# Edge masks read from five copies, a fetched tile in every sixth step, and the on-chip tile's keys behind its step's others

## The chip, the cores and the metric

The kernel runs on one core of a Trainium2 chip. The metric is device time of one launch in microseconds (us), the median of three runs. The profile is one execution more, with its own time. The core has five engines with queues of their own: TensorE (PE), VectorE (DVE), ScalarE (ACT), GpSimd (POOL) and SyncE (SP), and 16 DMA engines which carry the transfers that SP, ACT and POOL issue.

## The reference

A graph layer with five relation types: N = 3125 nodes, E = 100,000 edges sorted by destination, width 128, 8 heads. Each type has its own Q, K and V projections; the softmax runs over the edges of one type that share a destination.

```python
for r in range(R):
    mask = edge_types == r
    q = jnp.einsum('eh,khd->ekd', x_dst, W_Q[r])
    k = jnp.einsum('eh,khd->ekd', x_src, W_K[r])
    v = jnp.einsum('eh,khd->ekd', x_src, W_V[r])
    logits = (q * k).sum(-1) / scale + attn_bias[r][None, :]
    masked_logits = jnp.where(mask[:, None], logits, NEG)
    max_v = jax.ops.segment_max(masked_logits, dst, num_segments=n)
    ...
    exp_l = jnp.where(mask[:, None], jnp.exp(masked_logits - max_v[dst]), 0.0)
    sum_exp = jax.ops.segment_sum(exp_l, dst, num_segments=n)
    attn = exp_l / (sum_exp[dst] + 1e-12)
    out = out + jax.ops.segment_sum(attn[:, :, None] * v, dst, num_segments=n)
out = out.reshape(n, HIDDEN) @ out_proj_w.T + out_proj_b
h = out + node_embeddings
# layer norm of h with gamma and beta; then layernorm(x + that)
```

## The kernel before

Edges are taken in 196 groups of 512 (GE), a group in four tiles of 128 edges (T = 4, P = 128). The main loop has 66 steps (NST): two groups in the first and the last, three groups (12 tiles) in each of the 64 between. A step k also treats the first tile of step k+1, so that a block of 12 tiles (128 x 1536 values of K and as many of V) is one tile later than its groups.

The first 105 us or so prepare tables in HBM: kv_d (K and V of each node and type, a row of 1 KB), q_d (queries), key_d (which destination an edge has, as a number inside its window), and msk_d (a row of 642 bf16 marks for each group, by which the running maxima start anew at each destination; MW = 642). Then each step does the following.

- **POOL** gathers K and V of a tile of 128 edges with one indirect DMA (L849), into one of four buffers: step k into buffer k % 4, of which three lie in the tile kv_early and the fourth in kv_late. `point(k, j, leave)` stands at 11 places of a step (POINTS) and lets gathers go up to a number worked out from its place: 3.0 steps ahead (KV_LEAD) at the start of the program, falling to 2.0 at its end. `leave` is the instruction behind which they are let go.
- Two kinds of tiles aren't gathered. The first tile of steps 3 to 65 is made on chip: PE projects its nodes, and `early_keep` (L1109, ACT) copies the 128 x 256 result into the tile's place. And in one step of eight (PERIOD = 8: steps 11, 19, ..., 59, the table OWN_AT) one tile, `own`, is fetched row by row: `own_fetch` issues 16 DMAs of 1 KB (ROWS) on SP in each of the eight steps before, 128 in all for a tile, and `own_copy` (ACT, L883) puts it into place. The row's address is a register that SP loads from the table rows_at.
- **SP**, behind the products of step k (`take(k)`): `fetch_masks(k+2)` (tile mk, L936: three rows of msk_d, each to 40 partitions, one for each of five types and eight heads), `fetch_keys(k+3)` (tile kt, L719: 128 copies of the step's keys), `fetch_rows(k+3)` (tiles qw, L743: three windows of queries, at addresses that SP loads from the table window), then `own_fetch(k)`. All of them are on SP's one queue.
- **DVE**: products K x q of the step (L975), their sums by head (L1033), masks by type (L1008), norm of an earlier step (L1211 on), `weigh` (weights x V, L1160), the scans for the running maxima (L1115, L1119, which read mk), and `spot(k+2)` (L729), which compares kt with the row number and gives the one-hot matrix from which PE spreads the queries of step k+2 over its edges (L953).
- **PE** turns logits (L1065), spreads queries, turns weights, and sums weighted values by destination (L1194); **ACT** takes exponentials and makes the places matrices for the sums.

The order on each engine is the order in which the code stands (a manual schedule), with semaphores between the engines. A DMA that SP issues signals one of eight semaphores in turn; the next one that uses the same semaphore waits for it first.

Because the tile on chip is the first of the next step's buffer, it lies next to the 11 others only where step k and k+1 have neighbouring buffers. In 32 of the steps (k % 4 being 2 or 3) products and sums are two instructions each, one for 11 tiles and one for one tile.

Of the kernel before, what the change touches and what calls it, by code (L numbers as in the profile page):

```python
# [19 lines left out]
P = 128  # L20
# [3 lines left out]
R = 5  # L24
# [34 lines left out]
LANES = R * HEADS  # L59
L3 = G3 * LANES  # L60
# [8 lines left out]
PERIOD = 8  # L69
# [80 lines left out]
def windowed_path(  # L150
# [22 lines left out]
    msk_d = dram.tile([NGR, MW], BF16, name="msk_d")  # L173


    def keep(name, shape, dt=F32):
        return const.tile(shape, dt, name=name)
# [7 lines left out]
    rows_at = keep("rows_at", [HG, 2, P], I32)  # L185
# [11 lines left out]
    def kv_tile(name, n):  # L197
        pool = ctx.enter_context(tc.tile_pool(name=f"pool_{name}", bufs=1))
        return pool.tile([P, n * T * G3, KVW], F32, name=name)
# [361 lines left out]
    def own_rows():  # L561
        nc.vector.tensor_scalar_mul(rows_at, kvrow[:, :, P : 2 * P], float(KVW * 4))
# [100 lines left out]
    def late_x():  # L663
# [15 lines left out]
        11: [keys_b],  # L679
        12: [sorted_rows],  # L680
        13: [masks_a],
# [54 lines left out]

    def fetch_rows(k, leave=None):
        a, b = G0[k] + (k > 0), min(G0[k + 1] + 1, NGR)
        bytes_ = q_d.rearrange("n h -> (n h)").bitcast(U8)
        for g, f in zip(range(a, b), starts(window, a, b, SPE)):  # L740
            live["qw", g] = qw = ahead.tile([P, 3, H], BF16, name="qw", bufs=QWB)
            behind(
                nc.sync.dma_start(  # L743
                    qw.rearrange("p s h -> p (s h)").bitcast(U8),
                    bytes_[bass.ds(f, P * WINB)].rearrange("(p h) -> p h", h=WINB),
                ),
                leave,
            )

# [47 lines left out]
    begins()  # L797
    spills()
# [21 lines left out]

    def runs(a, b):
        out_ = []
        for q in range(a, b):
            k = AT[q // T][0]
            kv, at = place(k)
            at += q - T * G0[k]
            if out_ and out_[-1][0] is kv and out_[-1][2] == at:
                out_[-1][2] += 1
            else:
                out_.append([kv, at, at + 1])  # L830
        return out_
# [27 lines left out]
    def own_fetch(k):  # L859
        at = (k - 2) // PERIOD * PERIOD + PERIOD + 3  # L860
        if at not in OWN_AT:
            return
        i = (k - 2) % PERIOD * ROWS
        if i == 0:
            live["own", at] = flow.tile([P, KVW], F32, name="own")
        n = min(ROWS, P - i)
        g = OWN_AT[at] // T
        bytes_ = kv_d.rearrange("n h -> (n h)").bitcast(U8)
        _, rows = nc.values_load_multi_w_load_instructions(
            rows_at[g % HG : g % HG + 1, g // HG, i : i + n], engines=[SPE], min_val=0,  # L870
            max_val=(N * R - 1) * KVW * 4,
            skip_runtime_bounds_check_because="sources are nodes, types are relations",
        )
        for p, f in enumerate(rows, i):
            nc.sync.dma_start(
                live["own", at][p : p + 1].bitcast(U8).rearrange("o (a b) -> o a b", a=2),
                bytes_[bass.ds(f, KVW * 4)].rearrange("(o a b) -> o a b", o=1, a=2),
            )
# [52 lines left out]
    def fetch_masks(k, leave=None):  # L931
        n = len(groups(k))
        live["mk", k] = mk = flow.tile([L3, MW], BF16, name="mk", bufs=3)
        rows = msk_d[G0[k] : G0[k] + n]
# [3 lines left out]
                bass.AP(tensor=rows.tensor, offset=rows.offset, ap=[[MW, n], [0, LANES], [1, MW]]),  # L938
            ),
            leave,  # L940
        )
# [165 lines left out]
    def early_keep(k):  # L1107
        ((kv, c0, _),) = runs(B0[k + 1] - 1, B0[k + 1])
        nc.scalar.copy(kv[:, c0, :], live.pop("rows"))  # L1109
# [298 lines left out]
    fetch_rows(2)  # L1408

# [13 lines left out]
    for k in range(NST - 1):  # L1423
# [24 lines left out]
        if k < NST - 2:  # L1448
# [3 lines left out]
            if k >= 2:  # L1452
                own_fetch(k)
# [662 lines left out]
```

## Time and profile before

| | |
|---|---|
| Median of three runs | 1010.77 us (1009.69 to 1012.93) |
| The profiled execution: its time, its span | 1009.02 us, 1007.2 us |
| Granted TensorE clock, mean | 0.979 |
| Gathers on POOL (L849) | 712 |
| Fetches on SP of single rows (L875) | 896, of 1.0 KB |
| Moved by DMA | 189.60 MB, 188 GB/s |

The span is the time from the first to the last instruction in the trace. The profile gives busy time for each engine, groups of instructions by line, waits with what ended them, the DMA queues (q0 are POOL's gathers, q1 most of what SP issues), and a timeline. In a row of the timeline, the first number is the start, the second the duration (of several in a row, from the first's start to the last's end), and in brackets the idle time ahead of it. In a group's row, busy time and mean of one stand behind the first bar, idle time ahead of them and its causes behind the second.

### The profile page before, as it was taken

How to read it: one execution, taken by the hardware profiler on the slowest of the kernel's cores; microseconds unless marked ns; L12 is line 12 of the kernel's file. 1: busy time of each engine (PE TensorE's matmuls, PEld its weight loads, DVE VectorE, ACT ScalarE, POOL GpSimd, SP SyncE). 2: the span in 40 equal slices, each digit the busy share in tenths (PEclk: the TensorE clock that was granted, in tenths of full speed). 3: DMA queues.
4: the chain of work that ended last, by engine and by line, in shares of the span. 5: the costliest groups of instructions: out<-in, count | busy, mean ns of one | idle time of the engine just before them, and what ended most of it. 6: DMA issues, size and time to landing. Idle time of an engine off the chain costs nothing.

```text
span 1007.2 us, 23071 instructions
## 1 busy us (share of the span) xinstructions
PE 926.2 (92%) x6983; PEld 717.2 (71%) x6983; DVE 899.2 (89%) x1517; ACT 716.3 (71%) x1956; POOL 741.2 (74%) x793
## 2 busy tenths in 40 slices
PE   7995689999999999999999999999999999999986
PEld 3553577777777777777777777778777777777774
DVE  3666788999999999999999999999999999899997
ACT  2443377777787787778777777778777777777765
POOL 7777777777777777777777777777777777777760
PEclk9996799999999999999999999999999999999998
DMA  8997766567666666666666667665666765666630
GB/s 210 356 355 252 206 159 194 158 198 194 177 194 182 179 175 194 177 195 195 177 167 193 195 177 194 178 191 171 193 177 193 194 191 161 185 195 176 160 100 11
DMA packets 100547, 189.60 MB, mean 188 GB/s; under 512 B 19901, under 2 KB 61201, under 8 KB 100298
## 3 DMA queue, kind: packets, MB, share of 16 engines
q0 software_dynamic: 36192, 97.50, 34.9%
q1 hardware_dynamic: 63032, 89.66, 29.7%
q10 hardware_dynamic: 1194, 0.92, 0.4%
q8 instruction: 56, 0.92, 0.4%
q14 instruction: 73, 0.60, 0.2%
HBM read 157.61 MB, written 30.40 MB: 187 GB/s over the span
## 4 chain that ended last, share of the span: by engine, by line
DVE 39%; PE 24%; DMA 21%; issue 8%; POOL 4%; ACT 3%; DVEq 0%; POOLq 0%; ACTq 0%
DMA kv_early<-kv_d,idx 16%; DVE qe L1033 7%; DVE kv_early L975 6%; PE both L1194 5%; PE pr L514 4%; DVE wv L1160 4%; DVE run L1115 4%; DVE run L1119 3%; POOL kv_early L849 3%; PE qe L953 3%; DVE kv_late L975 2%; PE mid L1102 2%; DVE lx L1008 2%; DMA kv_late<-kv_d,idx 2%; PE lt L1092 2%
## 5 line engine op out<-in xcount | busy, mean ns | idle before, releaser
L849 POOL DMA_INDIRECT kv_early<-kv_d,idx x543 | 515.4, 949 | 166.6 <-issue 85.1
L1194 PE MATMUL both<-wv,at 128*125 128x136 f32 x1528 | 261.6, 296 | 0.0
L1173 ACT ACTIVATE at<-wide_at,nkey 128x125 f32<-128x125 f32 x776 | 245.0, 388 | 0.0
L1194 PEld LDWEIGHTS both<-wv,at 128*125 128x125 f32 x1528 | 201.8, 187 | 49.9 <-issue 44.4
L849 POOL DMA_INDIRECT kv_late<-kv_d,idx x169 | 160.0, 947 | 51.5 <-issue 27.1
L1102 PE MATMUL mid<-wkv,xr 128*128 128x256 f32 x630 | 146.5, 379 | 1.6 <-ACT xr L1096 1.6
L953 PE MATMUL qe<-qw,hot 128*128 128x128 bf16 x2349 | 146.1, 222 | 0.0
L953 PEld LDWEIGHTS <-hot 128*128 128x128 bf16 x2352 | 141.6, 102 | 0.5 <-DVE vio L650 0.4
L1102 PEld LDWEIGHTS mid<-wkv,xr 128*128 128x128 f32 x630 | 115.0, 190 | 15.0 <-ACT xr L1096 1.9
L1177 ACT ACTIVATE at<-at 128x500 f32<-128x500 f32 x194 | 120.3, 620 | 6.1
L975 DVE TENSOR_TENSOR kv_early<-kv_early,qe 128x1536 f32<-128x1536 f32 (+3 forms) x70 | 89.3, 1277 | 27.2 <-DMA kv_early<-kv_d,idx 22.0
L1115 DVE TENSOR_TENSOR_SCAN run<-mk,lt 120x640 f32<-120x640 bf16 (+1 forms) x66 | 97.6, 1478 | 1.5 <-PE lt L1065 1.5
L1259 ACT COPY oT<-fin 128x25 f32 x188 | 33.9, 180 | 81.9 <-PE fin L1255 77.9
L1119 DVE TENSOR_TENSOR_SCAN run<-lt,run 120x576 f32<-120x576 bf16 (+1 forms) x65 | 88.2, 1357 | 2.2
L1033 DVE TENSOR_REDUCE qe<-kv_early 128x96 f32<-128x1536 f32 (+2 forms) x65 | 86.7, 1334 | 2.2
L1160 DVE TENSOR_TENSOR wv<-kv_early,mid 128x1536 f32<-128x1536 f32 (+2 forms) x51 | 86.1, 1691 | 1.8 <-PE mid L1102 1.5
L1092 PE MATMUL lt<-diag,xg 128*128 128x512 f32 x252 | 83.5, 454 | 0.0
L1065 PE MATMUL lt<-ident,lx 128*120 128x128 f32 (+2 forms) x396 | 54.7, 275 | 24.6 <-DVE lx L1008 8.6
L1065 PEld LDWEIGHTS lt<-ident,lx 128*120 128x120 f32 (+2 forms) x396 | 38.5, 136 | 52.7 <-ACT diag L1086 20.2
L1144 PEld LDWEIGHTS mid<-gather_heads,ls 120*128 120x128 f32 (+1 forms) x528 | 64.2, 191 | 16.1 <-ACT xTq L901 12.1
L1144 PE MATMUL mid<-gather_heads,ls 120*128 120x24 f32 (+1 forms) x528 | 67.0, 265 | 9.4 <-ACT xTq L901 7.2
L1189 PE MATMUL both<-wv,over 128*5 128x136 f32 x380 | 75.3, 280 | 0.0
(232 smaller groups left out, 1341.5 us busy)
## 6 DMA issues: line engine op xcount, KB each, us to landing
kt<-key_d SPq DMA_DIRECT2D x64, 384.0 KB
qw<-q_d SPq DMA_DIRECT2D x196, 96.0 KB
kv_d<-kvs SPq DMA_DIRECT2D x24, 640.0 KB
own<-kv_d SPq DMA_DIRECT2D x896, 1.0 KB
q_d<-q SPq DMA_DIRECT2D x25, 480.0 KB
mk<-msk_d SPq DMA_DIRECT2D x64, 150.5 KB
kv_early<-kv_d,idx POOLq DMA_INDIRECT x543
kv_late<-kv_d,idx POOLq DMA_INDIRECT x169
```

Source lines behind the costliest of these rows:

```text
L849: nc.gpsimd.indirect_dma_start(out=kv[:, at, :], out_offset=None, in_=kv_d[:, :], in_offset=bass.IndirectOffsetOnAxis(ap=idx[:, q % T, q / ...
L953: spread = nc.tensor.matmul(dest[j], hot[:, j * P : (j + 1) * P], qw[:, c, :], start=(c == 0), stop=(c == 2),)
L975: made = nc.vector.tensor_tensor(kv[:, c0:c1, :H], kv[:, c0:c1, :H], qe[:, n:m], op=ALU.mult)
L1033: made = nc.vector.tensor_reduce(lg[:, n : n + c1 - c0], heads(kv[:, c0:c1, :H]), AX.X, ALU.add)
L1102: nc.tensor.matmul(rows, xr[:, r * P : (r + 1) * P], wkv[:, r].rearrange("h s c -> h (s c)"), start=(r == 0), stop=(r == R - 1),)
L1115: there = nc.vector.tensor_tensor_scan(run[:n], mk[:n, 1 : WIDE + 1], lt, -BIG, op0=ALU.add, op1=ALU.max)
L1119: back = nc.vector.tensor_tensor_scan(run[:n, SEG:][:, ::-1], masks[:, SEG:][:, ::-1], run[:n, SEG:][:, ::-1], -BIG, op0=ALU.add, op1=ALU.max,
L1144: nc.tensor.matmul(ex.rearrange("p (i t) k -> p t i k", t=T)[:, t], ls[: n * LANES, t * P : (t + 1) * P], gather_heads[: n * LANES, :n], s ...
L1160: return nc.vector.tensor_tensor(heads(wv[:, a:b, :H]), heads(kv[:, at + a : at + b, H:]), ex[:, a:b, :, None].to_broadcast([P, b - a, HEA ...
L1173: nc.scalar.activation(at[:, t, :], row_at[:, :WR], AF.Abs, bias=nkey[:, t, g : g + 1], scale=1.0)
L1177: return nc.scalar.activation(at[:, :n], at[:, :n], AF.Relu, bias=1.0, scale=-1.0)
L1194: nc.tensor.matmul(pp[:WR], at[:, t, :], wv[:, T * i + t, :], start=(t == 0), stop=(t == end))
```

## The change

Three edits.

1. A table many_d holds each group's masks five times over. In step 1, `copy_masks` issues one DMA on SP from msk_d to many_d, for all groups from step 6 on (COPIED): 179 rows read, 895 written, 1284 B each. From step 6 on, `fetch_masks` reads 15 rows of many_d, each to eight partitions, where it read three rows, each to 40.
2. PERIOD is 6: the tile fetched row by row is that of steps 9, 15, ..., 63 (ten), with 22 DMAs a step. SP's two loads of addresses in a step (three windows, 16 rows) become one, of a row of a new table at_step with 25 numbers, read by `load_step(k + 4)` behind the third row of the burst. The table is put together ahead of the loop, by a store to row_d and loads from it.
3. Each kv buffer has one column more. K of the tile made on chip is kept behind the others of its step (`beyond`), V where it was. `early_keep` makes two copies of 128 x 128 where these lie apart. `products` and `logits` are then one instruction in every inner step.

The core of the diff:

```diff
 LANES = R * HEADS
+COPIES = 5
+COPIED = 6
 L3 = G3 * LANES
...
 QWB = 10
...
 FAR = 4000
-PERIOD = 8
+PERIOD = 6
 ROWS = -(-P // PERIOD)
...
 KVA = 3
...
     msk_d = dram.tile([NGR, MW], BF16, name="msk_d")
+    many_d = dram.tile([NGR, COPIES, MW], BF16, name="many_d")
+    row_d = dram.tile([HG * 2 * P + P], I32, name="row_d")
...
     def keep(name, shape, dt=F32):
...
     window = keep("window", [1, NGR], I32)
-    rows_at = keep("rows_at", [HG, 2, P], I32)
+    at_step = keep("at_step", [NST, G3 + ROWS], I32)
     oT = keep("oT", [P, N + WN])
...
     gamma_t = keep("gamma_t", [P, H])
...
         pool = ctx.enter_context(tc.tile_pool(name=f"pool_{name}", bufs=1))
-        return pool.tile([P, n * T * G3, KVW], F32, name=name)
+        return pool.tile([P, n * T * G3 + 1, KVW], F32, name=name)
...
...
     def own_rows():
-        nc.vector.tensor_scalar_mul(rows_at, kvrow[:, :, P : 2 * P], float(KVW * 4))
+        rows_at = srt.rearrange("g s i -> g (s i)").bitcast(I32)[:, : 2 * P]
+        nc.vector.tensor_scalar_mul(
+            rows_at.rearrange("g (s i) -> g s i", s=2), kvrow[:, :, P : 2 * P], float(KVW * 4)
+        )
+        nc.sync.dma_start(
+            row_d[: HG * 2 * P].rearrange("(g i) -> g i", g=HG), rows_at
+        )
+
+    def own_steps(i):
+        def run():
+            for k in list(OWN_AT)[i::4]:
+                g = OWN_AT[k] // T
+                a, f = (g % HG * 2 + g // HG) * P, k - PERIOD - 1 + 3
+                nc.sync.dma_start(
+                    at_step[f : f + PERIOD, G3:],
+                    row_d[a : a + PERIOD * ROWS].rearrange("(i j) -> i j", j=ROWS),
+                )
+        return run
+
+    def window_steps():
+        nc.sync.dma_start(
+            at_step[3 : NST - 1, :G3],
+            window[:, G0[3] + 1 : G0[NST - 1] + 1].rearrange("o (k j) -> o k j", j=G3),
+        )
...
...
         10: [lambda: along(kvrow, 1, put_idx)],
-        11: [keys_b],
-        12: [sorted_rows],
-        13: [masks_a],
+        11: [keys_b, own_steps(0)],
+        12: [sorted_rows, own_steps(1)],
+        13: [masks_a, own_steps(2), own_steps(3)],
         14: [masks_b],
...
         16: [short_rows],
...
+    def load_step(k):
+        if not 3 <= k < NST - 1:
+            return
+        own = own_part(k - 3)
+        n = own[2] if own else 0
+        _, at = nc.values_load_multi_w_load_instructions(
+            at_step[k : k + 1, : G3 + n], engines=[SPE], min_val=0,
+            max_val=(N * R - 1) * KVW * 4,
+            skip_runtime_bounds_check_because="rows of nodes, sources and types",
+        )
+        live["at_step", k] = [
+            nc.s_assert_within(
+                f, 0, (N - 1) * R * WINB,
+                skip_runtime_bounds_check_because="destinations are nodes",
+            )
+            for f in at[:G3]
+        ] + list(at[G3:])
+
     def fetch_rows(k, leave=None):
...
         bytes_ = q_d.rearrange("n h -> (n h)").bitcast(U8)
-        for g, f in zip(range(a, b), starts(window, a, b, SPE)):
+        if 3 <= k < NST - 1:
+            at = live.pop(("at_step", k))
+            live["rows_at", k - 3] = at[G3:]
+        else:
+            at = starts(window, a, b, SPE)
+        for g, f in zip(range(a, b), at):
             live["qw", g] = qw = ahead.tile([P, 3, H], BF16, name="qw", bufs=QWB)
...
                 nc.sync.dma_start(
...
             )
+
+    def own_part(k):
+        at = (k - 2) // PERIOD * PERIOD + PERIOD + 3
+        if k < 2 or at not in OWN_AT:
+            return None
+        i = (k - 2) % PERIOD * ROWS
+        return at, i, min(ROWS, P - i)
...
...
     begins()
+    window_steps()
     spills()
...
     project_weights()
...
+    def beyond(k):
+        kv, at = place(k)
+        return kv, at + T * G3
+
     def runs(a, b):
...
             k = AT[q // T][0]
-            kv, at = place(k)
-            at += q - T * G0[k]
+            if q == T * G0[k] and k - 1 in early_at:
+                kv, at = beyond(k - 1)
+            else:
+                kv, at = place(k)
+                at += q - T * G0[k]
             if out_ and out_[-1][0] is kv and out_[-1][2] == at:
...
             else:
...
     def own_fetch(k):
-        at = (k - 2) // PERIOD * PERIOD + PERIOD + 3
-        if at not in OWN_AT:
+        rows = live.pop(("rows_at", k), None)
+        if not rows:
+            load_step(k + 4)
             return
-        i = (k - 2) % PERIOD * ROWS
+        at, i, n = own_part(k)
         if i == 0:
             live["own", at] = flow.tile([P, KVW], F32, name="own")
-        n = min(ROWS, P - i)
-        g = OWN_AT[at] // T
         bytes_ = kv_d.rearrange("n h -> (n h)").bitcast(U8)
-        _, rows = nc.values_load_multi_w_load_instructions(
-            rows_at[g % HG : g % HG + 1, g // HG, i : i + n], engines=[SPE], min_val=0,
-            max_val=(N * R - 1) * KVW * 4,
-            skip_runtime_bounds_check_because="sources are nodes, types are relations",
-        )
         for p, f in enumerate(rows, i):
+            if p == i + G3:
+                load_step(k + 4)
             nc.sync.dma_start(
...
                 bytes_[bass.ds(f, KVW * 4)].rearrange("(o a b) -> o a b", o=1, a=2),
...
         live["mk", k] = mk = flow.tile([L3, MW], BF16, name="mk", bufs=3)
-        rows = msk_d[G0[k] : G0[k] + n]
+        c = COPIES if k >= COPIED else 1
+        rows = (many_d if c > 1 else msk_d)[G0[k] : G0[k] + n]
         behind(
...
                 mk[: n * LANES, :],
-                bass.AP(tensor=rows.tensor, offset=rows.offset, ap=[[MW, n], [0, LANES], [1, MW]]),
+                bass.AP(
+                    tensor=rows.tensor, offset=rows.offset,
+                    ap=[[MW, n * c], [0, LANES // c], [1, MW]],
+                ),
             ),
             leave,
+        )
+
+    def copy_masks():
+        nc.sync.dma_start(
+            many_d[G0[COPIED] :],
+            msk_d[G0[COPIED] :, None, :].to_broadcast([NGR - G0[COPIED], COPIES, MW]),
         )
...
     def spread_q(k):
...
     def early_keep(k):
-        ((kv, c0, _),) = runs(B0[k + 1] - 1, B0[k + 1])
-        nc.scalar.copy(kv[:, c0, :], live.pop("rows"))
+        rows, (kv, c0), (to, c1) = live.pop("rows"), beyond(k), place(k + 1)
+        if kv is to and c0 == c1:
+            nc.scalar.copy(kv[:, c0, :], rows)
+        else:
+            nc.scalar.copy(kv[:, c0, :H], rows[:, :H])
+            nc.scalar.copy(to[:, c1, H:], rows[:, H:])
...
         n = len(groups(k)) * LANES
...
     fetch_rows(2)
+    load_step(3)
...
         if k + 2 < NST:
...
             take(k, made)
-            if k >= 2:
-                own_fetch(k)
+            own_fetch(k)
+            if k == 1:
+                copy_masks()
             point(k - 1, 7, weighted)
```

Instructions on SP, where the copy stands: step 1's last row fetches and step 2 up to its own rows, first before (L936 is the mask fetch, L875 the own rows).

```order
L936 DMA mk<-msk_d 120x1x642 [waits DMAHW1_49,DVE_49]
L719 DMA kt<-key_d 128x1536 [waits DMAHW2_49]
L704 TENSOR_LOAD window
L743 DMA qw<-q_d 128x768 [waits DMAHW3_49,PE_49]
L743 DMA qw<-q_d 128x768 [waits DMAHW4_49,PE_49]
L743 DMA qw<-q_d 128x768 [waits DMAHW5_49,PE_49]
L869 TENSOR_LOAD rows_at
L875 DMA own<-kv_d 1x1024 [waits DMAHW6_49]
```

And now (L998 is the mask fetch, L746 the keys, L793 the queries, L936 the own rows; a name like DMAHW5 is one of the eight semaphores):

```order
L769 TENSOR_LOAD at_step [waits DMAHW2_49]
L1009 DMA many_d<-msk_d 895x1x642 [waits DMAHW5_49]
L998 DMA mk<-msk_d 120x1x642 [waits DMAHW6_49,DVE_49]
L746 DMA kt<-key_d 128x1536 [waits DMAHW7_49]
L793 DMA qw<-q_d 128x768 [waits DMAHW0_49,PE_49]
L793 DMA qw<-q_d 128x768 [waits DMAHW1_49,PE_49]
L793 DMA qw<-q_d 128x768 [waits DMAHW2_49,PE_49]
L936 DMA own<-kv_d 1x1024 [waits DMAHW3_49]
L936 DMA own<-kv_d 1x1024 [waits DMAHW4_49]
L936 DMA own<-kv_d 1x1024 [waits DMAHW5_49]
L769 TENSOR_LOAD at_step
```

The copy stands ahead of step 2's fetches in SP's queue; its semaphore is the one that the third own row behind it waits for (DMAHW5), and the one load of addresses stands behind that row.

On DVE, the products and sums of step 2 and the instructions behind them, before:

```order
L975 TENSOR_TENSOR kv_early<-kv_early,qe 128x11x128
L975 TENSOR_TENSOR kv_late<-kv_late,qe 128x128
L1033 TENSOR_REDUCE qe<-kv_early 128x88
L1033 TENSOR_REDUCE qe<-kv_late 128x8
L1008 TENSOR_TENSOR lx<-qe,shut 128x3x4x40
```

and now (L1046 are the products, L1104 the sums):

```order
L1046 TENSOR_TENSOR kv_early<-kv_early,qe 128x12x128
L1104 TENSOR_REDUCE qe<-kv_early 128x96
L1079 TENSOR_TENSOR lx<-qe,shut 128x3x4x40
L1286 TENSOR_SCALAR both<-both 125x16
L1288 RECIPROCAL den<-both 125x16
```

Four instructions of 11 tiles and one have become two of twelve. Over the program DVE's queue has 2260 rows in place of 2324, ACT's 1809 in place of 1774.

## The prediction

> **What bounds the kernel now.** I read the page first: busy time, the DMA queues, the chain's shares, the costliest groups.
>
> ```profile
> span 1007.2 us, 23071 instructions
> PE 926.2 (92%) x6983; PEld 717.2 (71%) x6983; DVE 899.2 (89%) x1517; ACT 716.3 (71%) x1956; POOL 741.2 (74%) x793
> q0 software_dynamic: 36192, 97.50, 34.9%
> q1 hardware_dynamic: 63032, 89.66, 29.7%
> DVE 39%; PE 24%; DMA 21%; issue 8%; POOL 4%; ACT 3%; DVEq 0%; POOLq 0%; ACTq 0%
> L849 POOL DMA_INDIRECT kv_early<-kv_d,idx x543 | 515.4, 949 | 166.6 <-issue 85.1
> L849 POOL DMA_INDIRECT kv_late<-kv_d,idx x169 | 160.0, 947 | 51.5 <-issue 27.1
> ```
>
> PE and DVE have the largest busy shares, and the chain leans on DVE. But POOL's 74% hides a pattern: 712 gathers of 0.95 us, each with idle time ahead of it. So next the timeline of POOL, at the first gather, at the 69th and 70th, and near the end.
>
> ```profile
> 84.72 0.94 POOL L849 DMA_INDIRECT kv_early<-kv_d,idx  x1 [0.30 <-issue]
> 169.34 0.94 POOL L849 DMA_INDIRECT kv_early<-kv_d,idx  x1 [0.30 <-issue]
> 170.59 0.95 POOL L849 DMA_INDIRECT kv_early<-kv_d,idx  x1 [0.30 <-DVE kv_early L975]
> 974.49 0.94 POOL L849 DMA_INDIRECT kv_early<-kv_d,idx  x1 [1.33 <-DVE kv_early L975]
> 976.99 0.94 POOL L849 DMA_INDIRECT kv_early<-kv_d,idx  x1 [0.30 <-issue]
> ```
>
> A gather takes 0.95 us and 0.30 us of issue: 1.25 us from start to start (169.34 to 170.59). From first to last, (976.99 - 84.72)/711 = 1.255 us. So POOL is back to back for 892 us, whatever the busy share says, and DVE waits for what it lands (the waits):
>
> ```profile
> DVE kv_early L975 <- DMA kv_early<-kv_d,idx: 22.0, 24, 1.7
> DVE kv_early L975 <- DMA kv_late<-kv_d,idx: 2.7, 2, 1.6
> ```
>
> About 25 us in 26 waits, all under 2 us: DVE is a little faster than POOL and loses the difference there. The last of these waits is in the timeline of DVE for the end:
>
> ```profile
> 945.21 1.62 DVE L975 TENSOR_TENSOR kv_early<-kv_early,qe 128x1408 f32<-128x1408 f32 x1 [1.48 <-DMA kv_early<-kv_d,idx]
> 958.98 1.62 DVE L975 TENSOR_TENSOR kv_late<-kv_late,qe 128x1408 f32<-128x1408 f32 x1
> 970.18 0.68 DVE L975 TENSOR_TENSOR kv_early<-kv_early,qe 128x512 f32<-128x512 f32 x1
> ```
>
> The step at 945.21 (step 62) still waits for a gather; steps 63 to 65 don't. So POOL sets the time up to 945, DVE and PE the 62 us behind it. What shortens DVE before step 62 is worth nothing; a gather less before it is worth 1.25 us.
>
> **The change, part by part.** Sums are against the profiled execution, 1009.02 us with a span of 1007.2; the median of the runs is 1010.77, 1.75 more, which I add at the end.
>
> *Own tiles.* With a period of 6, the tiles fetched row by row are those of steps 9, 15, ..., 63 (10) in place of 11, 19, ..., 59 (7). Three gathers leave POOL. Up to step 62 it is nine against seven, so the gathers of that step land 2 x 1.25 = 2.5 us sooner. Cost on SP: 22 rows a step in place of 16. One cycle of SP:
>
> ```profile
> 485.04 0.75 SPq L936 DMA_DIRECT2D mk<-msk_d  x1
> 485.84 0.46 SPq L719 DMA_DIRECT2D kt<-key_d  x1
> 487.40 1.41 SPq L743 DMA_DIRECT2D qw<-q_d  x3
> 489.95 6.78 SPq L875 DMA_DIRECT2D own<-kv_d  x16
> 496.83 0.38 SPq L692 DMA_DIRECT2D q_d<-q  x1
> 497.87 0.74 SPq L936 DMA_DIRECT2D mk<-msk_d  x1
> ```
>
> 16 rows took 6.78 us, 0.42 each; six more are 2.5. The two register loads are the gaps 486.30 to 487.40 and 488.81 to 489.95, 1.1 us each; one of them goes, the other now stands behind the third row. From 485.04 to 497.21 SP is taken for 12.2 us, and would be for 12.2 + 2.5 - 1.1 = 13.6. A step of POOL is 11 gathers less one in six for the own tile, 10.83 x 1.25 = 13.6 us. So SP just fits. Part of the 0.42 is waiting for earlier landings, which doesn't grow with the rows, so I take it as hidden; the upper end is a rival. The ten more transfers of the preamble that set up the table lie on SP beside POOL's other gathers; I cost them at nothing, and the cover is small (84.72 must not move). If they held the first gather, the loss would be theirs one for one: up to 10 x 0.46 us (a transfer's issue at 485.84) = 4.6.
>
> *On-chip keys.* These rows are DVE by shape:
>
> ```profile
> L1033 DVE TENSOR_REDUCE qe<-kv_early 128x96 f32<-128x1536 f32 x31 | 54.6, 1761 | 1.1
> L975 DVE TENSOR_TENSOR kv_early<-kv_early,qe 128x1536 f32<-128x1536 f32 x31 | 54.4, 1753 | 16.9 <-DMA kv_early<-kv_d,idx 14.6 <-ACT xTq L901 1.2 <-issue 1.0
> L1033 DVE TENSOR_REDUCE qe<-kv_late 128x88 f32<-128x1408 f32 x16 | 26.0, 1627 | 0.6
> L975 DVE TENSOR_TENSOR kv_late<-kv_late,qe 128x1408 f32<-128x1408 f32 x16 | 25.9, 1619 | 1.9 <-DMA kv_late<-kv_d,idx 0.7 <-DMA kv_early<-kv_d,idx 0.6 <-issue 0.4
> L1033 DVE TENSOR_REDUCE qe<-kv_late 128x8 f32<-128x128 f32 x16 | 4.7, 295 | 0.6
> L975 DVE TENSOR_TENSOR kv_late<-kv_late,qe 128x128 f32<-128x128 f32 x16 | 4.5, 280 | 0.0
> ```
>
> A split step costs 1619 + 280 + 1627 + 295 = 3821 ns, a whole one 1753 + 1761 = 3514: 0.31 us less in 32 steps, 9.8 us of DVE. But up to step 62 that goes into the waits for gathers; only the steps in the tail (62 and 63) give it, 2 x 0.31 = 0.6 us. ACT pays with two copies for one in 32 steps:
>
> ```profile
> L1109 ACT COPY kv_early<-mid 128x256 f32<-128x256 f32 x47 | 16.6, 353 | 0.0
> L901 ACT COPY xTq<-mid 128x128 f32<-128x128 f32 x21 | 5.5, 264 | 5.0 <-PE mid L896 3.6
> ```
>
> 2 x 264 - 353 = 0.18 us a step, on an engine busy for 71%: nothing.
>
> Without the masks the sum is -2.5 - 0.6 = **-3.1 us**.
>
> *Masks.* From step 6 on, a step's masks are read from five copies. What a fetch loads on the DMA engines shows a stretch that has no other transfer on q1 (the DMA view, 281.65 to 283.1):
>
> ```profile
> q0 software_dynamic: 16, 0.05, 57.1%
> q1 hardware_dynamic: 76, 0.08, 17.6%
> ```
>
> 0.176 x 16 = 2.8 engines carry it, though it writes 120 partitions: it has three source rows. With 15 it would take more engines and land sooner; nothing in the waits stands on mk, so that is worth nothing, or a little less delay of gathers beside it, which POOL's pace hides.
>
> The price is the copy itself: one transfer in step 1, 895 rows of 1284 B, 1.149 MB, in SP's queue. [...] The page's q1 moves 89.66 MB in 0.297 x 16 x 1007.2 = 4786 engine-us, 18.7 KB/us; so 1149/18.7 = 61 us. (The window gives 0.08 MB/(0.176 x 16 x 1.45) = 19.6 KB/us, 59 us.) Spread over 16 engines it would be 3.8 us. [...]
>
> [...]
>
> Who stands behind it? SP in step 2 and DVE in steps 3 and 4:
>
> ```profile
> 118.78 0.77 SPq L936 DMA_DIRECT2D mk<-msk_d  x1
> 119.61 0.41 SPq L719 DMA_DIRECT2D kt<-key_d  x1
> 121.12 1.31 SPq L743 DMA_DIRECT2D qw<-q_d  x3
> 131.45 0.77 SPq L936 DMA_DIRECT2D mk<-msk_d  x1
> 132.28 0.41 SPq L719 DMA_DIRECT2D kt<-key_d  x1
> 153.25 0.90 DVE L729 TENSOR_SCALAR hot<-kt,row_of 128x512 bf16<-128x512 bf16 x3
> 155.41 1.75 DVE L975 TENSOR_TENSOR kv_early<-kv_early,qe 128x1536 f32<-128x1536 f32 x1 [0.93 <-DMA kv_early<-kv_d,idx]
> ```
>
> The copy is issued at about 123, behind step 1's qw. Step 2's mk, kt and qw (131.45 on) follow in the same queue; each has some rows on the engine that the copy holds, and a transfer has landed only with its last row. The third row of step 2's own burst also waits for the copy's semaphore. That kt is of step 5, and DVE needs it at 153.25, in step 3. The copy ends at 123 + 61 = 184 if alone; then kt's rows and the spot, 0.9 + about 3 us: 188. Meanwhile DVE stands, and POOL may go only so far ahead: its gathers are let go by the products of the step (releaser at 170.59). The last one that step 3 lets go is the one at 169.34; the next needs products(4), which stand behind the spot. So POOL loses 188 - 170.6 = 17.4 us. DVE is later by 188 - 154.15 = 34 us, of which 17 are its lead, and wins that back over 60 steps from the slack of its 25 us of waits and the 9.8 us above. The end moves by 17.4 - 3.1 = **+14.3 us**.
>
> Bounds of this term: at 24 KB/us (a quarter above the mean) the copy ends at 171 and the spot at 175, a loss of 4.4 and a sum of +1.3; if gathers take a third of that engine, as q0's 34.9% says, the copy lasts up to 61/0.65 = 94 us and the sum is about +47. The gathers' own shares on it are small and mean-rate figures hold such sharing already, so I stay near 61.
>
> Queue order on the engine is what makes kt wait. [...] Were it otherwise, the sum would be -3.1, as in the second case below.
>
> **Rivals.** (a) *The copy is spread, or overtaken, and nothing stalls*: the only case that ends faster. For it: 179 rows on the source side are many; the steps before 153.25 have 30 us of slack from 123, and POOL has 47. Against: the 2.8 engines. It decides at a copy of about 43 us, so two engines would do. Then -3.1: 1009.02 to 1005.9, a median of 1007.7. (b) *SP becomes the bound*: its 13.6 us of work meets a step of 13.6. Each 0.1 us over costs 6 us in 60 steps; at 13.75, with no stall, +9 - 3 = about +6 to 8: 1017 to 1019. For it: the cycle's sum has no slack. Against: the rows' waits, which don't grow. (c) *A short stall*, spot done between 171 and 177: the gain and the loss cancel, within 3 us of before. (d) *Landings*: with lighter mask fetches gathers land sooner (21% of the chain is DMA). POOL's pace bounds it at 3 x 1.25 = 3.8; it adds less than 1 us to (a).
>
> **How the numbers follow.** About 0.3%, 3 us, is what a measurement of this kernel can tell from no change. The stall on one engine has 0.66: 1009.02 + 14.3 = 1023.3, plus 1.75 is 1025; its own range is 1015 to 1036. (a) with (d) 0.22, of which 0.13 passes 3 us; (b) 0.06; (c) 0.06. Slower: 0.66 + 0.06 less 0.04 for stalls that come out short, 0.68; faster 0.14; same 0.18. To leave out no more than 2 in 10 the range must hold (a): 1006.5 to 1036.
>
> **What would show it.** In the profile after: the row of the copy's landing, tens of us, at a steady 15 to 25 GB/s of additional flow on 1/16 of the engines; in step 3 of DVE a wait of some 34 us of the spot for kt; on POOL one gap of some 17 us near 170, and none elsewhere; 709 gathers with 1.25 us between; L1046 with 1536 elements in all inner steps; the mask fetch on some 14 engines. If DVE has no wait at 153, the one-engine reading is wrong and (a) holds. If POOL shows gaps in all steps and SP none, it is (b).

## The result: 34 us slower, and the profile after

| | before | after |
|---|---|---|
| Median | 1011.02 us (1009.16 to 1012.93, 6 runs) | 1044.76 us (1042.57 to 1047.13, 6 runs) |
| Span of the profiled execution | 1007.2 us | 1040.8 us |

The ratio is 1.0332, 95% interval 1.0311 to 1.0353. The page of the changed kernel, the lines that answer to those of before:

```profile
span 1040.8 us, 23779 instructions
PE 932.5 (90%) x6983; PEld 727.6 (70%) x6983; DVE 891.2 (86%) x1453; ACT 717.5 (69%) x1991; POOL 738.4 (71%) x790
q0 software_dynamic: 36048, 97.11, 32.7%
q1 hardware_dynamic: 65706, 91.32, 27.2%
PE 39%; DVE 29%; DMA 12%; SPq 7%; issue 6%; ACT 4%; POOL 2%; DVEq 0%; ACTq 0%; POOLq 0%
L756 DVE TENSOR_SCALAR hot<-kt,row_of 128x512 bf16<-128x512 bf16 x196 | 61.1, 367 | 51.4 <-DMA kt<-key_d 48.3
```

DVE works 8 us less (891.2 for 899.2; 9.8 were counted); no engine works much more (PE 6 us). SP's queue has entered the chain with 7%, and the spot has waited 48.3 us for keys. Where, the timelines of SP, DVE and POOL around the copy say:

```profile
124.95 0.73 SPq L1009 DMA_DIRECT2D many_d<-msk_d  x1
132.94 51.62 SPq L998 DMA_DIRECT2D mk<-msk_d  x1
184.60 2.16 SPq L746 DMA_DIRECT2D kt<-key_d  x1
188.90 12.68 SPq L936 DMA_DIRECT2D own<-kv_d  x22
195.42 0.88 DVE L756 TENSOR_SCALAR hot<-kt,row_of 128x512 bf16<-128x512 bf16 x3 [39.63 <-DMA kt<-key_d]
170.67 0.95 POOL L914 DMA_INDIRECT kv_early<-kv_d,idx  x1 [0.30 <-issue]
196.57 0.94 POOL L914 DMA_INDIRECT kv_early<-kv_d,idx  x1 [24.95 <-DVE hot L756]
```

The copy is issued at 124.95. SP's next DMA, step 2's mask fetch, doesn't merely wait on the engines: its issue takes 51.62 us, and SP stands. The keys of step 5 go out at 184.60, the spot runs at 195.42, and POOL loses 24.95 - 0.30 = 24.65 us at the place that was forecast. The DMA view of 174 to 184, when POOL stood and the copy was nearly alone on q1:

```profile
DMA packets 168, 0.22 MB, mean 22 GB/s; under 512 B 2, under 2 KB 166, under 8 KB 168
q1 hardware_dynamic: 164, 0.21, 6.4%
```

0.064 x 16 = 1.02 engines: the copy had one, at 21 KB/us; beside gathers it ran slower (in 150 to 160, 0.17 MB, 17 KB/us).

Once they were issued, the keys still had to wait on that engine. By the trace's DMA records, 120 of their 128 rows had started by 189.7; the last eight ran from 193.86 to 194.85, behind the copy's last 119 rows (776 of the 895 had started by 184.56, when the mask fetch's issue ended) and, by an estimate from the 2.8 engines of such a fetch, 40 of the mask fetch's 120. The DMA view of 191.5 to 193.8 shows one engine again (0.066 x 16 = 1.06):

```profile
q1 hardware_dynamic: 41, 0.05, 6.6%
```

The copy's first row moved at 128.58, 3.6 us behind its issue. Taking 40 rows at its pace off 193.86, its last moved at about 191.5 (an estimate): 63 us, 18 KB/us on the whole.

But that is not all. ScalarE and POOL near 270, the largest of eight smaller gaps that POOL has between 240 and 290, 9.1 us in all beyond the usual 0.30:

```profile
268.63 0.41 ACT L944 COPY kv_early<-own 128x256 f32<-128x256 f32 x1 [7.09 <-DMA own<-kv_d]
271.90 0.94 POOL L914 DMA_INDIRECT kv_late<-kv_d,idx  x1 [5.21 <-ACT at L1252]
```

ScalarE waits 7.09 us for the tile of step 9, which SP fetched row by row and late; what stands behind it on ScalarE lets POOL's next gathers go. And POOL's first and last gathers:

```profile
85.96 0.94 POOL L914 DMA_INDIRECT kv_early<-kv_d,idx  x1 [2.15 <-DMA kt<-key_d]
1010.14 0.95 POOL L914 DMA_INDIRECT kv_early<-kv_d,idx  x1 [0.30 <-issue]
```

The last is 33.15 us later than before (976.99). That is +1.24 at the first (84.72), +24.65, +9.1, +1.35 at one gap near the end (2.68 against 1.33), -3.75 for three gathers: 32.6, and 0.6 of smaller things.

### The profile page after: what moved, and what is told of

Read it like the earlier page. It is cut to its first block, busy times and chain, and to the rows that moved or that the text cites. A ratio compares the mean times of both kernels' runs of the same rounds, so it can differ in the third digit from the quotient of the medians.

```text
span 1040.8 us, 23779 instructions
## 1 busy us (share of the span) xinstructions
PE 932.5 (90%) x6983; PEld 727.6 (70%) x6983; DVE 891.2 (86%) x1453; ACT 717.5 (69%) x1991; POOL 738.4 (71%) x790
## 4 chain that ended last, share of the span: by engine, by line
PE 39%; DVE 29%; DMA 12%; SPq 7%; issue 6%; ACT 4%; POOL 2%; DVEq 0%; ACTq 0%; POOLq 0%
PE both L1269 9%; PE qe L1024 5%; PE mid L1173 5%; DVE qe L1104 5%; PE pr L518 4%; PE lt L1163 3%; DVE kv_early L1046 3%; DVE run L1190 3%; PE mid L1219 3%; SPq L936 3%; DVE run L1194 3%; SPq L998 3%; DMA kv_early<-kv_d,idx 3%; PE both L1264 2%; DMA qw<-q_d 2%
## 5 line engine op out<-in xcount | busy, mean ns | idle before, releaser
L914 POOL DMA_INDIRECT kv_late<-kv_d,idx x171 | 162.6, 951 | 58.0 <-issue 27.1
L1173 PE MATMUL mid<-wkv,xr 128*128 128x256 f32 x630 | 150.2, 386 | 37.4 <-ACT xr L1167 37.4
L1173 PEld LDWEIGHTS mid<-wkv,xr 128*128 128x128 f32 x630 | 117.5, 194 | 51.9 <-ACT xr L1167 37.9
L1024 PE MATMUL qe<-qw,hot 128*128 128x128 bf16 x2349 | 148.9, 224 | 0.0
L1024 PEld LDWEIGHTS <-hot 128*128 128x128 bf16 x2352 | 144.6, 103 | 0.5 <-DVE vio L677 0.4
L756 DVE TENSOR_SCALAR hot<-kt,row_of 128x512 bf16<-128x512 bf16 x196 | 61.1, 367 | 51.4 <-DMA kt<-key_d 48.3
L1046 DVE TENSOR_TENSOR kv_early<-kv_early,qe 128x1536 f32<-128x1536 f32 (+4 forms) x54 | 86.7, 1606 | 6.3 <-DMA kv_early<-kv_d,idx 4.9
L1104 DVE TENSOR_REDUCE qe<-kv_early 128x96 f32<-128x1536 f32 (+2 forms) x49 | 84.1, 1716 | 1.6
L1136 PE MATMUL lt<-ident,lx 128*120 128x128 f32 (+2 forms) x396 | 54.8, 276 | 18.3 <-DVE lx L1079 10.2
```

Source lines behind the costliest of these rows:

```text
L914: nc.gpsimd.indirect_dma_start(out=kv[:, at, :], out_offset=None, in_=kv_d[:, :], in_offset=bass.IndirectOffsetOnAxis(ap=idx[:, q % T, q / ...
L1024: spread = nc.tensor.matmul(dest[j], hot[:, j * P : (j + 1) * P], qw[:, c, :], start=(c == 0), stop=(c == 2),)
L1046: made = nc.vector.tensor_tensor(kv[:, c0:c1, :H], kv[:, c0:c1, :H], qe[:, n:m], op=ALU.mult)
L1104: made = nc.vector.tensor_reduce(lg[:, n : n + c1 - c0], heads(kv[:, c0:c1, :H]), AX.X, ALU.add)
L1173: nc.tensor.matmul(rows, xr[:, r * P : (r + 1) * P], wkv[:, r].rearrange("h s c -> h (s c)"), start=(r == 0), stop=(r == R - 1),)
```

## The experiments

Every ratio is against the kernel before on the same chip; it is not the quotient of the two medians, which can differ from it by some tenths of a percent. On four of the chips used TensorE's granted clock was 0.87 to 0.90; the kernel before took 1312 to 1337 us there, and a step of the changed kernels 17.3 to 18.3 us in place of some 13.6. PE has the largest part of the chain there, by the page of the copy of 176 rows:

```profile
PE 58%; issue 11%; another core or an unknown queue 10%; DVE 10%; ACT 9%; POOL 1%; DMA 1%; DVEq 0%; ACTq 0%; POOLq 0%
```

PE's own busy time is up by only some 13% there (1048.8 us in that run, 926.2 before), the time by 30%; what makes up the rest is open. The table marks these runs; what can be told from them is where SP and DVE stand, not a gain of 0.3%.

| Kernel | This | Before | Ratio (95%) | Step |
|---|---|---|---|---|
| copy of 176 rows | 1007.35 | 1009.96 | 0.997 (0.9958 to 0.9982) | 13.5 |
| two copies of each mask | 1012.65 | 1010.4 | 1.0022 (1.0002 to 1.0042) | 13.2 |
| slow copy, period 8 | 1038.77 | 1009.96 | 1.0291 (1.0276 to 1.0307) | 13.3 |
| no copy | 1043.63 | 1009.96 | 1.0319 (1.0286 to 1.0351) | 14.0 |
| keys alone | 1011.34 | 1009.96 | 0.9999 (0.9984 to 1.0015) | 13.6 |
| low clock: copy of 176 rows, twice | 1309.41, 1316.43 | 1315.57, 1311.9 | 0.9971, 1.0049 (to 1.0091) | 17.7, 17.6 |
| low clock: no copy, twice | 1314.45, 1316.86 | 1315.57, 1311.9 | 1.0002, 1.005 (to 1.0088) | 17.9 |
| low clock: copy of 158 rows | 1317.31 | 1315.57 | 1.0015 (0.9978 to 1.0051) | |
| low clock: copy from ScalarE | 1334.13 | 1315.57 | 1.0181 (1.0119 to 1.0243) | |
| low clock: slow copy, period 8 | 1337.55 | 1311.9 | 1.0264 (1.0171 to 1.0356) | |
| low clock: period alone | 1321.39 | 1311.9 | 1.0116 (1.0062 to 1.017) | |
| low clock: copy of 176 rows, period 8 | 1315.52 | 1312.33 | 1.0033 (0.9996 to 1.0071) | |
| low clock: no copy, period 7, three times | 1322.53, 1338.08, 1342.67 | 1312.33, 1332.38, 1336.57 | 1.0066, 1.0013, 1.0031 | 18.2 |

The steps are means from one mask fetch's issue to the next behind 250 us, in the profile (18.2 is the second run's).

### The copy of 176 rows

```diff
-COPIED = 6
+COPIED = 7
```

Expected of three runs, the first two of which fell on a chip with a low clock (0.9971, and 1.0049 with an interval of 1.0008 to 1.0091: no stall, and no gain where PE leads the chain; theory S's 3 us were not to be had there):

> The changed kernel with one number changed: the copies begin at step 7, so that 176 rows are read and 880 written (176 and 880 have 16 as a common divisor; 179 and 895 have only 1). Theory S (one engine carried the copy, SP's queue stood behind it, and every later delay follows from that): the copy takes about 68/16, some 4 to 6 us; DVE waits under 2 us for the keys in step 3, POOL has no gap of over 3 us between 170 and 300, and the time is 1011.0 - 3 = 1008, between 1006 and 1010. Rival R (the 24.7 us gap is the copy's, but the 9 us of gaps between 240 and 290 come from 22 row fetches a step): about 1011 + 9 - 3 = 1017. Rival C (any copy of this size costs, by its traffic): above 1025.

> The changed kernel with the copies begun at step 7 (176 rows, 16 engines), on another run of the chip, since the first chip's TensorE clock was so low (0.88) that PE and not POOL set the time there. Theory S, if POOL sets the time of before again: 3 us under before (POOL's gaps of 250 us in total gone, last gather about 2.5 to 4 us sooner than before's); rival R (22 rows a step cost by themselves): 6 us over before; rival 0: within 1 us of before.

> The changed kernel with the copies begun at step 7 (176 rows, 16 engines). Theory S (all of the loss is the copy's length on one engine, and what is late behind it): 1010.5 - 3 = 1007.5, within 1.5; no wait of ScalarE over 1 us for the tile of step 9. Rival R (22 rows a step make the tile of step 9 late even so): ScalarE waits 3 to 7 us for it, DVE 2 to 5, and the time is within 2 us of before, no gain.

Measured in the third: 2.6 us under before; ScalarE never waits for a fetched tile. SP and POOL in this kernel:

```profile
125.61 0.63 SPq L1009 DMA_DIRECT2D many_d<-msk_d  x1
137.02 0.77 SPq L998 DMA_DIRECT2D mk<-msk_d  x1
86.61 0.94 POOL L914 DMA_INDIRECT kv_early<-kv_d,idx  x1 [0.52 <-issue]
975.70 0.94 POOL L914 DMA_INDIRECT kv_early<-kv_d,idx  x1 [0.30 <-issue]
```

The issue of the next fetch takes 0.77 us in place of 51.62. One number, three groups less to copy, takes away the whole loss and is faster than both kernels (1007.35 us). The copy's rows moved in some 8 us: on q1, 0.65 MB from 126 to 130 and 0.63 MB from 130 to 136, in the second stretch with 8.3 engines' time (0.517 x 16), of the copy's 1.13 MB. That it had 16 engines was the author's estimate; no view counts them. Between first and last gather are 889.1 us, where before had 892.3, 3.2 less. The first gather is 1.9 us later; the preamble's new transfers are the likely reason (see the last point but one on the prediction).

### The copy shorter, from the same 179 rows

```diff
-COPIES = 5
+COPIES = 2
```

> The changed kernel with two copies of each mask in place of five (358 rows of 1284 B written, 179 read, still one engine; a fetch reads six rows, 20 times each). Theory L (the loss is the copy's length on its engine less the lead that POOL has): 358/895 x 68 = 27 us, the copy ends 27 us behind its issue, SyncE's next fetch is issued up to 17 us late, the keys of step 5 land before DVE wants them or up to 8 us late, POOL has no gap over 3 us there, and ScalarE waits under 1 us for the tile of step 9. The time is that of the version with 16 engines within 3 us. Rival K (what costs is that one engine is taken at all, or that 179 rows share no divisor): still a gap of 15 us or more on POOL, and a time 20 us or more over before.

Two copies of each mask, 358 rows. SP and DVE:

```profile
134.95 13.12 SPq L998 DMA_DIRECT2D mk<-msk_d  x1
161.37 0.88 DVE L756 TENSOR_SCALAR hot<-kt,row_of 128x512 bf16<-128x512 bf16 x3 [4.84 <-DMA kt<-key_d]
```

SP is held 13 us, DVE 4.84, and between its first gather and 976 POOL has no gap over 1 us. So it is the copy's length against the lead, not the 179 rows as such. But it wasn't the time of the copy of 176 rows (5 us more), and the expectation on step 9 fell: ScalarE waited 6.68 us there (the profile names a mask fetch as what ended it), and 9.4 us in six waits for fetched tiles later.

### The copy of 158 rows

```diff
-COPIED = 6
+COPIED = 13
```

> The changed kernel with the copies begun at step 13: 158 rows read (2 x 79), 790 written: two engines. Theory S: 790 x 1284 B on two engines at 17 KB/us each take 30 us, the copy ends at about 156, the keys of step 5 land at about 158 to 162; DVE waits for them some 3 to 6 us in step 3, but POOL is let go before it would stand (170), so no gap over 2 us near 170; the time is 1007 to 1012. Rival C (traffic, not its place on the engines): 1025 and more. Rival R: about 1017.

Low clock, where 170 and 156 don't hold. SP's next fetch was held 12.91 us (175.44 to 188.35) and DVE didn't wait for keys. No loss that can be measured (1.0015), as theory S has it; that two engines carried the copy wasn't shown.

### The copy in ScalarE's queue

```diff
     def copy_masks():
-        nc.sync.dma_start(
+        nc.scalar.dma_start(
```

> The changed kernel with the same 179-row copy issued by ScalarE in place of SyncE, at the same place of the code; one engine carries it for 60 to 70 us again. Theory Q (the order inside one queue is what made the keys wait): mask, key and query fetches of step 2 are issued within 3 us of their place, the keys of step 5 land within 5 us, no wait of DVE over 5 us in step 3, and the time is 1007 to 1013. Rival E (the engine itself is taken, whichever queue the copy is in): the keys' rows on that engine stand behind the copy as before, and the time is 1035 to 1045.

Low clock. Neither theory was right. Step 2's mask, key and query fetches went out in their places and their keys were there in time (theory Q so far), but the step's own rows didn't. SP's timeline and its waits:

```profile
178.42 2.55 SPq L793 DMA_DIRECT2D qw<-q_d  x3
181.70 63.97 SPq L936 DMA_DIRECT2D own<-kv_d  x22
SPq L936 <- DMA many_d<-msk_d: 53.7, 1, 53.7
```

The third row uses the copy's semaphore and waited 53.7 us for it, with SP's whole queue behind; one step later DVE waited 23.98 us for keys all the same, and POOL stood 21.26 us. So the long copy held SP in two ways: in SP's own queue the issue of what came next took 51.62 us, and from ScalarE's queue the own row that takes the copy's semaphore waited 53.7 us. In the changed kernel the first came first.

### The slow copy with period 8

```diff
-PERIOD = 6
+PERIOD = 8
```

> The changed kernel, copy on one engine, with period 8 in place of 6 (16 rows a step, first fetched tile in step 11). Theory T (the 9 us of gaps between 240 and 290 come of SP being late when the tile of step 9 is fetched, with 22 rows a step to make up): one gap of about 25 us near 170 to 197, ScalarE waits under 1 us for the fetched tile, under 3 us of other gaps, and the time is before + 24 to 27 = 1035 to 1038. Rival U (those gaps belong to DVE's catching up, whatever the period): they stay at 7 to 10 us, and the time is 1043 to 1048.

That run, at a low clock, had the gap (22.05 us) and no wait for a fetched tile, but its time says nothing of theory T's sum. Again at a step of 13.3 us:

> The changed kernel, copy on one engine, with period 8 in place of 6. Theory T (the 9 us of gaps between 240 and 290 come of SP being late with the tile of step 9): one gap of about 25 us on POOL, ScalarE waits under 1 us for the tile of step 11, under 3 us of other gaps there, a time of before + 24 to 27 = 1035 to 1038. Rival U (DVE's catching up, whatever the period): 7 to 10 us of gaps, 1043 to 1048.

Measured 28.8 us over before, a little above the range (the profiled execution, the fastest of its four, took 1034.83). POOL:

```profile
195.22 0.94 POOL L914 DMA_INDIRECT kv_early<-kv_d,idx  x1 [24.95 <-DVE hot L756]
277.04 0.94 POOL L914 DMA_INDIRECT kv_early<-kv_d,idx  x1 [0.81 <-ACT wv L1229]
```

The same gap, and hardly any of the 9 us behind it; ScalarE never waits for a fetched tile. With the copy of 176 rows they are gone, too. So they come of both together: SP late by the copy, and period 6, with 22 rows a step and its first tile in step 9. Which of these two counts isn't separated, since period 8 changes both (16 rows, first tile in step 11).

### No copy

```diff
-COPIES = 5
+COPIES = 1
...
-            if k == 1:
-                copy_masks()
```

> The changed kernel without the copy: masks are read as three rows, 40 times each, in all steps; period 6 and the keys' place stay. Theory S: as with the copy on 16 engines, 1008, within 2 us of it, since nothing waits for the masks. Rival R: 1017. Rival M (masks on 15 engines leave the gathers' transfers more room): this kernel is slower than the one with the copy on 16 engines by 2 us or more.

> The changed kernel without the copy, masks read as three rows 40 times in all steps. Theory S: as with 16 engines, within 1.5 us. Rival M (reading 15 rows is worth something by itself): slower than with 16 engines by 2 us or more.

These two, at a low clock, gave 1.0002 and 1.005, as the copy of 176 rows did beside them (0.9971 and 1.0049). Then:

> The changed kernel without the copy, masks read as three rows 40 times in all steps. Theory S: the time of the version with 16 engines within 1.5 us. Rival M (reading 15 rows is worth something by itself): slower than that by 2 us or more.

This was the surprise: 33.7 us over before with no copy at all. Rival M, 2 us or more, has the sign, and says nothing of such a size. Who ScalarE waited for before it put a fetched tile in place, the worst such wait, and SP's waits:

```profile
  DMA own<-kv_d: 33.4, 6
  DMA mk<-msk_d: 8.4, 2
  DMA kv_early<-kv_d,idx: 7.1, 1
821.62 0.40 ACT L944 COPY kv_late<-own 128x256 f32<-128x256 f32 x1 [8.95 <-DMA own<-kv_d]
SPq L936 <- DMA kt<-key_d: 38.5, 52, 1.6
SPq L936 <- DMA qw<-q_d: 23.2, 61, 1.4
SPq L998 <- DVE kv_early L1046: 12.5, 2, 9.1
SPq L936 <- DMA mk<-msk_d: 6.2, 14, 1.3
```

and SP's waits of the copy of 176 rows:

```profile
SPq L998 <- DVE kv_early L1046: 32.0, 19, 10.7
SPq L936 <- DMA qw<-q_d: 10.4, 18, 2.0
SPq L936 <- DMA kt<-key_d: 3.3, 6, 1.2
```

and those of its own rows in the kernel before (L875 there):

```profile
SPq L875 <- DMA kt<-key_d: 42.8, 52, 1.5
SPq L875 <- DMA qw<-q_d: 31.5, 85, 1.1
SPq L875 <- DMA mk<-msk_d: 14.6, 27, 1.4
```

Own rows wait for the eight semaphores that masks, keys and queries of the step hold: 67.9 us without the copies, 13.7 with them, 0.9 a step. From a mask fetch's issue to the last own row, SP took 12.0 us a step before (16 rows), 13.7 without copies (22 rows) and 12.65 with them (22 rows), against steps of 13.6, 14.0 and 13.5. The reading that fits is that without copies SP is full, its tiles come late, and ScalarE, which waits for them (8.95 us at 821.62, 33.4 us in six waits), holds what stands behind. SP's slack shows in the wait for DVE's products ahead of its mask fetch: 19 times with the copy of 176 rows, twice without.

This reading has two supports more: with period 8 (16 rows) the absence of copies costs nothing (keys alone, 1.0), and at a step of nearly 18 us, on the chips with a low clock, no copy and the copy of 176 rows can't be told apart (1.0002 and 0.9971; 1.005 and 1.0049), and ScalarE never waits for a fetched tile. Period 7 was to be the third:

> No copy, masks as three rows 40 times, period 7 (19 rows a step, 8 fetched tiles), keys behind the others. Theory F (SyncE's queue was full): 3 x 0.43 = 1.3 us less of SyncE's work a step than the 13.7 of period 6, 12.4 against a step of 13.6; ScalarE waits under 2 us in all for fetched tiles, no gaps of POOL over 1.5 us before 970, and the time is 1009 to 1011, within 2 us of before. Rival G (a copy being there, or the alignment of period and steps, matters in some other way): over 1020.

> No copy, masks as three rows 40 times, period 7 (19 rows a step, 8 fetched tiles), keys behind the others. Theory F (SyncE's queue was full at period 6): 3 x 0.43 = 1.3 us less of SyncE's work a step than the 13.7 of period 6, 12.4 against a step of 13.6; ScalarE waits under 2 us in all for fetched tiles, no gaps of POOL over 1.5 us before 970, and the time is within 2 us of before. Rival G (a copy being there, or the alignment of period and steps, matters in some other way): 10 us or more over before.

> No copy, masks as three rows 40 times, period 7 (19 rows a step, 8 fetched tiles), keys behind the others. Theory F (SyncE's queue was full at period 6): 3 x 0.43 = 1.3 us less of SyncE's work a step than the 13.7 of period 6, 12.4 against a step of 13.6; ScalarE waits under 2 us in all for fetched tiles, no gaps of POOL over 1.5 us before 970, and the time is within 2 us of before. Rival G (a copy being there, or the alignment of period and steps, matters in some other way): 10 us or more over before.

All three runs of it fell on chips with a low clock, where the loss was 0.1 to 0.7% and ScalarE never waited for a fetched tile; SP had room there at period 6 as well. So at a step of 13.6 us it stays open whether fewer rows alone are enough, or the alignment of period and steps matters.

### Keys alone

The changed kernel with no copy and period 8.

> The keys of the tile on chip behind the others of its step, with period 8 and no copy (the addresses still come as one table of 19 numbers a step). By the prediction's working: 9.8 us less of DVE's work, of which only the last two steps' 0.6 us comes through: 0.0 to 1.2 us under before. Rival D (DVE's pace and not POOL's sets more of the time than the waits show): 3 us or more under before.

Measured 1011.34 against 1009.96, ratio 0.9999: nothing that can be told. DVE shows why: between 250 and 970 it works 5.9 us less (673.15 against 679.08) and waits 6.6 us more (27.9 against 21.3). The work saved became waiting, as forecast. But the gathers are named for only 0.8 of the 6.6 (19.4 against 18.6); ScalarE, which copies twice now, is named for 6.6 in all against 1.2. The profile infers these names, so what the waiting was for isn't shown.

### The period alone, and the copies alone

Period 6 with neither copies nor the keys' new place:

> Period 6 with its one table of addresses, without the copies and with the on-chip tile's keys where they were (products and sums in two pieces in 32 steps). Theory S: three gathers less, 2.5 us under before, and 0.6 less than the version with the keys moved. Rival R: 6 us over before. Rival P (the ten loads of the table hold the first gather): the first gather of K and V starts 1 us later than before and the gain is 1 us less.

At a low clock: 1.2% slower than before, where the same with the keys moved was 0.5% slower. The two intervals overlap (1.0062 to 1.017, 1.0013 to 1.0088), and none of the three theories was about that pace; whether products in two pieces cost something there isn't shown.

The copy of 176 rows, from step 7 on, with period 8:

> Copies on 16 engines from step 7, keys behind the others, period 8 (16 rows, 7 tiles as before). Theory F: SyncE has room with or without the copies, POOL sets the time with as many gathers as before; within 1.5 us of the kernel before and of the version with the keys alone. Rival M (masks landing sooner are worth something beside SyncE's room): 2 us or more under before.

At a low clock too: 1.0033 (0.9996 to 1.0071), no difference that can be measured, as theory F has it, though at a pace at which it says little.

## Why the prediction was wrong, point by point

- **The bound** was right: POOL's gathers at 1.25 us set the time. 709 of them took 889.1 us from first to last where nothing stalled.
- **The copy on one engine, the order behind it and the place of the stall** were right: one engine, spot in step 3, gather at 170. The 61 us are those of one engine; that the copy goes on one no row of before shows, it was the author's estimate, and the run after showed 1.02 engines and some 63 us in its place. The order in the queue, for which the prediction had no row, is borne out: the keys' last eight rows (193.86 to 194.85) moved behind the copy's and the mask fetch's, and with the copy in ScalarE's queue the same keys came in time.
- **The size of the stall** was too small, 24.65 for 17.4. The transfer itself was nearly right, some 63 us for 61. But its first row moved at 128.58, where the sum began at 123, and 40 rows of step 2's mask fetch (the estimate above), 2.3 us at that pace, stood ahead of the keys. The spot was done at 196.30 for 188; the last gather before the gap stood 1.3 us later than forecast, too (170.67 for 169.34). That SP was held for 51.62 us was not foreseen; for these keys it probably changed little, since their last rows would have stood behind the copy anyway; no run tells the two apart.
- **The step that failed** is "one gap of some 17 us near 170, and none elsewhere". Behind the stall the prediction followed DVE and POOL, and not SP. By its own sum SP "just fits", 13.6 us of work in a step of 13.6, so an SP that comes out of the copy some 50 us late can't win that back; it put this at nothing. The runs showed 9.1 us more of gaps on POOL, with ScalarE waiting 7.09 us for the tile of step 9. With 22 rows and no long copy they are gone, with the long copy and period 8 all but 0.5. Of the 19 us between +14.3 and +33.7, the stall's size has 7.3, this step 9.1, the first gather 1.2 and the gap near the end 1.4.
- **The masks** at nothing, "nothing in the waits stands on mk", was wrong, too, though that isn't what made this kernel slow. Only DVE's, PE's and POOL's waits had been looked at. SP's own had 14.6 us for mk, 42.8 for kt and 31.5 for qw in the kernel before, 88.9 us in all; with the copy of 176 rows 13.7 are left. "Without the masks the sum is -3.1" was measured as +33.7 (no copy, period 6). Rival (b) had this mechanism, SP as the bound: its 13.6 us of work came out at 13.7, and the rows' waits didn't grow, as it said (67.9 us). But the step became 14.0 us where it was costed at 13.75, and it was given 6 in 100.
- **The gain without a stall**, -3.1, was measured as -2.6 (interval -4.2 to -1.8), and rival (a) would have been right had the table begun at step 7. That is luck in part: the gain is there only because the copies gave SP the room that the prediction took for granted.
- **The ten transfers of the preamble**, costed at nothing: the first gather came 1.2 to 1.9 us later in the four profiles with ten of them (at a granted clock of 0.95 or more), 0.2 and 0.8 later in the two with seven, at period 8. That fits the transfers as the cause, but no run varied them alone; the bound of 4.6 held it.
- **The keys' place** is worth nothing that can be measured, as forecast.

## What to carry to other kernels

See how many engines carry a large DMA, and how long, before you place it: the copy of 179 rows had one for some 63 us, that of 176 was through in some 8, and that was some 36 us of a 1 ms kernel. What sets the number these runs don't show. Price a transfer not only by who reads it, but by who next needs its engine, its queue and its semaphore (51.62 us of SP by the queue here, 53.7 by the semaphore), and when you find a stall, follow every queue out of it: SP, with no slack, still held ScalarE for 7.09 us near 270 here. And read the waits of the queue that issues DMAs like those of an engine: here it had 1.6 us of slack a step, and an edit that looked idle was what kept the other one from filling it.

## What the runs showed of the hardware

- SP's issue of the mask fetch behind the copy took 51.62 us with 895 rows written from 179, 13.12 with 358 from 179, 12.91 with 790 from 158 (at a low clock), and 0.77 with 880 from 176. The 51.62 us ended when 119 rows of the copy were still to start.
- A mask fetch from three source rows had 2.8 engines (before, 281.65 to 283.1), the copy from 179 rows 1.02 (after, 174 to 184).
- One engine moved rows of 1284 B at 21 KB/us alone (after, 174 to 184), and at 17 KB/us while gathers ran beside it (150 to 160).
- The same program took 1010 us at a granted clock of 0.97 to 0.98, and 1312 to 1337 on four chips at 0.87 to 0.90. A change that shows at one pace can vanish at the other: no copy cost 3.2% at the first, 0.0 and 0.5% at the second.
